# A recurrent gate beside a mixture of experts on one core: router in one run, low-rank product on VectorE, sigmoids into PSUM, first tokens on two queues

## The chip, the core and the metric

The kernel runs on one core of one Trainium2 chip. The metric is device time in microseconds, from runs of the whole program; the median of three runs of the kernel before is 840.8 us (840.55 to 841.84). A separate execution under the hardware profiler took 842.09 us.

Five engines work beside each other, each through its own row of instructions in program order: TensorE (PE in the profile, its weight loads PEld), VectorE (DVE), ScalarE (ACT), GpSimd (POOL) and SyncE (SP), which issues most transfers. They meet at semaphores. All data is 32-bit float.

## The reference

The input is 4 x 1024 tokens of 1024 values. Every token is normalised, then used twice: by a gated recurrence over the tokens of a batch entry, and by a feed-forward part with a router whose output is scattered to 8 rows. The results are multiplied and added to the input.

```
xn = layernorm(x)
# recurrence
g    = sigmoid(xn @ gate_w.T + gate_b)
u_g  = xn * g
d_lr = mean_t(u_g) @ d_lr_u @ d_lr_v / R        # R = 4
s    = G * cumsum(b * u_g / G),  G = cumprod(tanh(a))
y    = c * s + (d + d_lr) * u_g
# feed-forward
idx, gates = top 2 of softmax(xn @ wr.T), 8 experts
h    = silu(silu(xn @ w1.T) @ w3.T) @ w2.T
out  = zeros.at[idx[:, k]].add(gates[:, k] * h)  for k = 0, 1
result = x + y * silu(out)
```

The index of the scatter is the number of the expert, 0 to 7. So only the first 8 rows of the output differ from x, and the kernel needs y for these alone: the gate product is made for the first 1024 tokens only, whose mean `d_lr` wants, and all other rows of x are copied.

## The kernel before, in words

Tokens go in four groups (`sb` 0 to 3) of 1024. For each group there are products named by kind: `u` (by w1), `m` (by w3), and for group 0 also `g` (by the gate weights). Each product of 1024 x 1024 x 1024 is made by Strassen's scheme on 2 x 2 halves, with seven half products `i` = 1 to 7, and each of those again by seven small ones (`Half.step`, line 813), unless it is listed as plain (`PLAIN_G`, `PLAIN_M`), when it takes eight. A small product is four instructions of 128 x 256 into a PSUM bank (`small`, line 763), tagged X, Z or Y. TensorE does little else, while GpSimd and VectorE make the sums and differences of operands and VectorE and ScalarE take the results out of PSUM.

The order is written out by hand. `line` (lines 195 to 204) lists the half products; each gets a place (`start`), and a small product stands every two places. Everything else is put at a place with `at(place, f)` (line 176), and `run_todo` emits what is due before each small product. A function that yields a number goes on that many places later. All engines' instructions go through the class `Pinned`, which keeps them in this order on their engine; so the profile gives line 89 for nearly all of them, and one reads it by the names of tiles.

Memory: 20 blocks `b` of 128 x 2048 and 18 quarters `q` of 128 x 512 in SBUF, handed round by counts of uses. PSUM has two X banks, two Z banks, one Y bank, one small bank (`ps_sm`), and in `ps_acc` the bank `acc` of the scatter and one bank `rows`.

The parts that the change touches:

- First tokens. `load_x0` brings 256 tokens of x to SBUF, token by row, in four pieces for the first block (line 1070). `stats0` (line 236) takes mean and variance by `bn_stats`, makes diagonal matrices of means and scales, and after a lag spreads them to all partitions by products with ones (`bc`). `norm0` (line 287) then normalises the transposed tokens xT in place. `stats0(0, 0)` has a lag of 0: its products stand ahead of the first small product. Before it TensorE runs 16 products of no use (`idle`, line 1067).
- First weights. `first_weights` (line 559) loads block (0, 0) of w1 in two halves, interleaved with two pieces of xT; the block of gw is one transfer behind the second x block.
- Router. `route` (line 380) makes the logits of a group: 8 slices of the contraction x 4 parts of tokens, each a product 32 columns wide, into bank `plT`. It yields after every second slice. For group `sb` it begins at place U[5] + 2 (group 0) or U[5] - 4, U[5] being the start of half product 5 of `u`.
- Scatter. `scatter` (line 932) adds the gated rows of h of a group into `acc`; it is put six places behind the last result that it needs (line 926).
- Gating. `gated` (line 951) takes a quarter of g at a time: ScalarE's sigmoid in place, two places later VectorE's product with xn, which also gives sums for the mean.
- Differences by a spare bank. `with_bank` (line 512) has ScalarE copy one operand to `acc` or to a bank `rows`, so that VectorE's difference reads PSUM.
- Low-rank product. `recurrence` (line 982) makes the mean, then `pr` (8 products on TensorE), then `pd` (8 more), and all of y. It begins at place 25 of group 1. `rows` (line 1169) transposes y by products with the identity (`ty`) and begins 40 places before the end.

Of the kernel before, what the change touches and what calls it, by code (L numbers as in the profile page):

```python
# [10 lines left out]
F32 = mybir.dt.float32  # L11
# [5 lines left out]
P = 128  # L17
# [5 lines left out]
def kernel(  # L23
# [101 lines left out]
    NB, NQ = 20, 18  # L125
    IDLE = 16
    blocks = deque(
# [18 lines left out]
    pool.memset(eps, EPS)  # L146

    root = const.tile([P, 1], F32, tag="root", name="root")
    act.activation(root, eps, AF.Sqrt)
# [11 lines left out]
    vec_sb = const.tile([P, 5, KD], F32, tag="vec", name="vec_sb")  # L161
    lru_sb = const.tile([P, KD, R], F32, tag="lru", name="lru_sb")


# [71 lines left out]
    def stats0(I, a, xb, lag):  # L236

        mv = sp.tile([P, 2, 2], F32, tag="mv", name=f"mv_{I}{a}")
        for tt in range(2):
            xt = xb[:, 2 * tt : 2 * tt + 2, :]  # L240
            bn = sp.tile([P, 2, nc.vector.BN_STATS_DIM], F32, tag=f"bn{tt}", name=f"bn_{I}{a}{tt}")
            for n in range(2):
                dve.bn_stats(bn[:, n, :], xt[:, n, :])
            dve.bn_aggr(mv[:, tt, :], bn)
        xb.drop()
        sd = sp.tile([P, 2], F32, tag="sd2", name=f"sd_{I}{a}")
        act.activation(sd, mv[:, :, 1], AF.Sqrt, bias=eps)
        dg = quarter()

        def diagonals(s, w):  # L250
            for tt in range(2):
                dve.tensor_scalar(
                    dg[:, (2 * s + tt) * P : (2 * s + tt + 1) * P],
                    ident,
                    w[:, tt : tt + 1],
                    None,
                    ALU.mult,
                )

        diagonals(0, mv[:, :, 0])  # L260
        v = sp.tile([P, 2], F32, tag="v2", name=f"v_{I}{a}")
        dve.tensor_scalar(v, mv[:, :, 1], EPS, None, ALU.add)
        rs = sp.tile([P, 2], F32, tag="rs", name=f"rs_{I}{a}")
        scales(rs, v, sd, 2)
        diagonals(1, rs)
        if (I, a) == (1, 1):
            bc = ps_sm.tile([P, 2, Q], F32, tag="sm", name="bc_11")
        elif (I, a) == (1, 0):
            bc = ps_y.tile([P, 2, Q], F32, tag="Y", name="bc_10")
        elif a == 1:  # L270
            bc = acc.rearrange("p (s n) -> p s n", s=2)
        else:
            bc = ps_acc.tile([P, 2, Q], F32, tag="rows", name="bc_00")
        yield lag
        for s in range(2):
            pe.matmul(
                bc[:, s, :],
                ones,
                dg[:, s * Q : (s + 1) * Q],
                start=True,  # L280
                stop=True,
                skip_group_check=True,
            )
        dg.drop()
        bc0[I, a] = bc

    def norm0(I, a, J, parts=1):
        p = part(xn[0, I, J], a)
        bc = bc0[I, a]
        w = 4 // parts  # L290
        for h in range(0, 4, w):
            for s, op in ((0, ALU.subtract), (1, ALU.mult)):
                row = bc[:, s : s + 1, :].to_broadcast([P, w, Q])
                dve.tensor_tensor(p[:, h : h + w, :], p[:, h : h + w, :], row, op)

# [84 lines left out]
    def route(sb):  # L380
# [3 lines left out]
        for k in range(KD):  # L384
            J, b, kt = k // 4, k // 2 % 2, k % 2
            for g in range(4):
                I, a = g // 2, g % 2
                pe.matmul(
                    plT[g * CG : (g + 1) * CG, :],
                    wr_sb[:, k, :],  # L390
                    xn[sb, I, J][:, 2 * a + b, kt * Q : (kt + 1) * Q],
                    start=(k == 0),
                    stop=(k == KD - 1),
                )
            if k % 2:
                yield 1
        for IJ in HB:
# [60 lines left out]

    def load_w(name, KN, uses, before=()):
        t = block(uses)  # L460
        if not before:
            sync.dma_start(t.tile, weights[name][KN])
        for b, f in enumerate(before):
            f()
            sync.dma_start(t[:, b::2, :], weights[name][KN][:, b::2, :])
        return t
# [42 lines left out]

    spare = [0]  # L510

    def with_bank(out, p, q):

        def copy(j):
            spare[0] += 1
            ps = acc if spare[0] % 2 else ps_acc.tile([P, H], F32, tag="rows", name="spare")
            act.copy(ps, q[:, j])  # L520
            return ps

        ps = copy(0)
        yield 0.5
        for j in range(4):
            ahead = copy(j + 1) if j < 3 else None
            dve.tensor_tensor(out[:, j], p[:, j], ps, ALU.subtract)
            ps = ahead
            yield 0.5

    def late_sums(name, i):
# [26 lines left out]

    def first_weights(kind, name, before=()):

# [4 lines left out]

        b = {}

        def load(key, KN, uses, *before):
            b[key] = load_w(name, KN, uses, *before)

# [39 lines left out]
        off = 0 if kind == "u" else 1  # L610
        load(1, (0, 0), 2, before)
        one()
# [301 lines left out]
    def done(kind, sb, I, J, q, c):  # L914
# [5 lines left out]
        elif kind == "m":  # L920

            act.activation(c[:, q], c[:, q], AF.Silu)
            if q == 2:
                h2[I, J] = c
                if sb < NS - 1 and (I, 1 - J) in h2:
                    at(here[0] + 6, scatter, sb, [(I, 0), (I, 1)])
        elif q == 2:
            at(here[0] + 1, gated, sb, I, J, c)
# [22 lines left out]
    def gated(sb, I, J, c):  # L951

        xb = xn[sb, I, J]
        for b in range(2):
            for mt in range(2):
                m = J * 4 + b * 2 + mt

                def piece(t):
                    return t.tile.rearrange("p (a b) (m n) -> p a b m n", b=2, n=Q)[:, :, b, mt, :]

                act.activation(piece(c), piece(c), AF.Sigmoid, bias=vec_sb[:, 4, m : m + 1])
                yield 2
                dve.scalar_tensor_tensor(
                    piece(c),
                    piece(c),
                    1.0,
# [4 lines left out]
                )  # L971
                yield 0.5
        if sb == 0 and I == 0:
# [8 lines left out]
    def recurrence():  # L982

        av, bv, cv, dv = (vec_sb[:, i, :] for i in range(4))
        lrv = block()
        lrv_sb = lrv.tile.rearrange("p a n -> p (a n)")[0:R, 0:D]
        sync.dma_start(lrv_sb, lr_v)
        um = const.tile([P, KD], F32, tag="um", name="um")
        dve.tensor_reduce(um, usum, AX.X, ALU.add)
        dve.tensor_scalar(um, um, 1.0 / T, None, ALU.mult)  # L990
        yield 4
        pr = ps_sm.tile([R, 1], F32, tag="sm", name="pr")
        for k in range(KD):
            pe.matmul(pr, lru_sb[:, k, :], um[:, k : k + 1], start=(k == 0), stop=(k == KD - 1))
        yield 3
        rk = const.tile([R, 1], F32, tag="rk", name="rk")
        dve.tensor_copy(rk, pr)
        yield 4
        pd = ps_sm.tile([P, KD], F32, tag="sm", name="pd")
        for m in range(KD):  # L1000
            pe.matmul(pd[:, m : m + 1], lrv_sb[:, m * P : (m + 1) * P], rk, start=True, stop=True)
        lrv.drop()
        yield 3
        deff = const.tile([P, KD], F32, tag="deff", name="deff")
# [47 lines left out]
    def consts():  # L1052
        sync.dma_start(wr_sb, wr)
        sync.dma_start(vec_sb, vecs)
        sync.dma_start(lru_sb, lr_u)

    def copy_rows(n):
# [7 lines left out]


    idle = ps_sm.tile([P, P], F32, tag="sm", name="idle")
    for _ in range(IDLE):
        pe.matmul(idle, ones, ident, start=True, stop=True, skip_group_check=True)
    load_x0(0, 0, 4)  # L1070
    first = block(USES[0, 0] + G[0, 0])
    xn[0, 0, 0] = first
    first_weights(
        "u",
        "w1",
        [
            lambda b=b: sync.dma_start(first[:, b, :], xT[0, 0, 0, :, b, :])
            for b in range(2)
        ],
    )  # L1080
    load_x0(0, 1)
    first_weights("g", "gw")
    sync.dma_start(first[:, 2:4, :], xT[0, 0, 0, :, 2:4, :])
    at(-27, load_x0, 1, 0)
    at(-26, load_x0, 1, 1)
    at(-25, load_xn, 0, 0, 1, USES[0, 1] + G[0, 1])
    at(-16, load_xn, 0, 1, 0, USES[1, 0] + G[1, 0])
    at(-15, load_xn, 0, 1, 1, USES[1, 1] + G[1, 1])
    at(-10, lambda: stats0(0, 0, x0[0, 0], 0))
    at(-9, norm0, 0, 0, 0, 2)  # L1090
    at(-8, lambda: stats0(0, 1, x0[0, 1], 12.5))
    at(-7, lambda: stats0(1, 0, x0[1, 0], 14))
    at(4.6, norm0, 0, 1, 0)
    at(4.7, lambda: stats0(1, 1, x0[1, 1], 7.5))
    at(4.8, norm0, 0, 0, 1)
    at(5, norm0, 0, 1, 1)
    at(8, norm0, 1, 0, 0)
    at(11, norm0, 1, 0, 1)
    at(15, norm0, 1, 1, 0)
# [18 lines left out]
    for sb in range(NS):  # L1118
# [5 lines left out]
        at(U[3] - (12 if sb == 0 else 8.6), s4, "u", sb, n)  # L1124
        at(U[5] + (2 if sb == 0 else -4), route, sb)
        M = {i: start["m", sb, i] for i in range(1, 8)}
# [7 lines left out]
        if sb + 1 < NS:  # L1134
# [5 lines left out]
            for IJ in HB:  # L1140
# [5 lines left out]
                )  # L1146
    at(start["u", 1, 1] + 25, recurrence)
    first_w3()
# [121 lines left out]

    at(END - 40, rows)
    at(start["m", NS - 1, 7] + 15, scatter, NS - 1, [(0, 0), (1, 1)])
# [90 lines left out]
```

## Time and profile before

| | |
|---|---|
| median of three runs | 840.8 us |
| profiled execution | 842.09 us |
| its span, first to last instruction | 840.3 us |
| mean granted TensorE clock | 0.997 |
| TensorE busy | 828.4 us, 4143 records |
| VectorE busy | 546.2 us, 889 |
| GpSimd busy | 490.4 us, 377 |
| ScalarE busy | 242.7 us, 390 |
| transfers | 194.97 MB, mean 232 GB/s |

How to read it: times are from the span's start. A row of the timeline has start, length, engine, line, operation, the tile written and those read, shapes and a count of merged instructions; in brackets stands how long the engine was idle before, and what ended that. One 32-bit product instruction leaves two records, so `x8` is one small product. Records of products overlap, so costs on TensorE are read from start to start. SPq is SyncE's row of transfer issues; releasers are inferred from semaphores.

### The profile page before, as it was taken

What the parts mean: (1) busy time and instruction counts of PE and PEld (TensorE: products, weight loads), DVE (VectorE), ACT (ScalarE), POOL (GpSimd) and SP (SyncE); (2) the same over time, 40 slices, a digit from 0 to 9 for tenths busy, and PEclk for the clock granted to TensorE, in tenths of its full rate; (3) what the DMA queues carried; (4) which work ended last, traced back from release to release, by engine and by line L of the source; (5) the groups of instructions that cost most, each with busy time, mean ns of one, the idle gap of its engine ahead of it and who ended that gap; (6) DMA issues with size and microseconds to landing.
All of it is one profiled execution on the core that took longest, in us unless ns stands there. A gap on an engine that the chain in (4) does not pass through costs nothing.

```text
span 840.3 us, 11334 instructions
## 1 busy us (share of the span) xinstructions
PE 828.4 (99%) x4143; PEld 702.4 (84%) x4143; DVE 546.2 (65%) x889; ACT 242.7 (29%) x390; POOL 490.4 (58%) x377
## 2 busy tenths in 40 slices
PE   7999999999999999999999999999999999999997
PEld 6887888888888868888888778888888688888885
DVE  6966699888579427676897225774994246655643
ACT  0214205866121207442112225531122021220111
POOL 0379888784878768546355753743458453564500
PEclk9999999999999999999999999999999999999999
DMA  8945427622995889728966757639775646546700
GB/s 334 422 152 210 158 97 298 239 98 79 384 402 202 303 270 378 288 87 317 410 225 227 271 180 287 238 133 404 304 237 180 197 168 245 192 144 218 287 13 2
DMA packets 55679, 194.97 MB, mean 232 GB/s; under 512 B 6356, under 2 KB 9668, under 8 KB 43592
## 3 DMA queue, kind: packets, MB, share of 16 engines
q1 hardware_dynamic: 55592, 194.24, 62.7%
q8 instruction: 33, 0.54, 0.3%
q14 instruction: 22, 0.18, 0.1%
q10 hardware_dynamic: 32, 0.02, 0.0%
HBM read 171.10 MB, written 39.87 MB: 251 GB/s over the span
## 4 chain that ended last, share of the span: by engine, by line
PE 92%; DMA 3%; DVE 2%; POOL 1%; issue 1%; SPq 0%; ACT 0%; POOLq 0%; DVEq 0%
PE X_u L89 23%; PE X_m L89 20%; PE Z_u L89 12%; PE Z_m L89 11%; PE Y_u L89 6%; PE X_g L89 6%; PE Y_m L89 5%; PE Z_g L89 4%; PE acc L89 2%; PE plT L89 2%; DMA b<-in_w 2%; DVE b L89 1%; DMA w<-q 1%; POOL q L89 1%; PE Y_g L89 1%
## 5 line engine op out<-in xcount | busy, mean ns | idle before, releaser
L89 POOL TENSOR_TENSOR q<-b 128x512 f32<-128x512 f32 x144 | 198.5, 1391 | 230.7 <-DVE b L89 52.5
L89 ACT ACTIVATE b<-b 128x512 f32<-128x512 f32 (+1 forms) x152 | 105.0, 696 | 316.2 <-DVE b L89 311.4
L89 DVE TENSOR_TENSOR b<-b,b 128x512 f32<-128x512 f32 x160 | 155.6, 989 | 2.9
L89 POOL TENSOR_TENSOR q<-b,q 128x512 f32<-128x512 f32 x91 | 130.2, 1433 | 8.8 <-issue 6.7
L89 POOL TENSOR_TENSOR b<-b,b 128x512 f32<-128x512 f32 x72 | 94.8, 1342 | 35.8 <-PE X_u L89 26.4
L89 DVE TENSOR_TENSOR b<-X_u,b 128x512 f32<-128x512 f32 x87 | 59.9, 689 | 72.2 <-PE X_u L89 71.5
L89 PE MATMUL X_u<-q,q 128*128 128x256 f32 x432 | 103.0, 381 | 0.0
L89 DVE TENSOR_TENSOR b<-X_m,b 128x512 f32<-128x512 f32 x84 | 57.4, 687 | 63.7 <-PE X_m L89 63.5
L89 PE MATMUL X_m<-q,q 128*128 128x256 f32 x416 | 98.5, 380 | 0.0
L89 PEld LDWEIGHTS X_u<-q,q 128*128 128x128 f32 x432 | 81.3, 190 | 14.9 <-POOL q L89 1.7
L89 POOL TENSOR_TENSOR q<-q,b 128x512 f32<-128x512 f32 x53 | 71.9, 1358 | 34.5 <-PE X_u L89 28.8
L89 PEld LDWEIGHTS X_m<-q,q 128*128 128x128 f32 x416 | 78.8, 190 | 11.8 <-issue 0.8
L89 DVE TENSOR_TENSOR b<-b,bc 128x1024 f32<-128x1024 f32 (+1 forms) x62 | 72.8, 1178 | 6.3 <-ACT bc L89 5.3
L89 PE MATMUL X_m<-b,b 128*128 128x256 f32 x272 | 63.8, 380 | 0.8 <-POOL b L89 0.8
L89 PE MATMUL X_u<-b,b 128*128 128x256 f32 x248 | 60.4, 388 | 2.8 <-DVE b L89 2.5
L89 PEld LDWEIGHTS X_m<-b,b 128*128 128x128 f32 x272 | 51.3, 190 | 8.6 <-POOL b L89 1.2
L89 PEld LDWEIGHTS X_u<-b,b 128*128 128x128 f32 x248 | 48.1, 195 | 10.7 <-DVE b L89 3.3
L89 PE MATMUL X_u<-b,q 128*128 128x256 f32 x216 | 51.3, 380 | 0.0
L89 PE MATMUL Y_u<-b,b 128*128 128x256 f32 x216 | 51.3, 380 | 0.0
L89 PE MATMUL Z_u<-q,b 128*128 128x256 f32 x216 | 51.3, 380 | 0.0
L89 PE MATMUL Z_u<-q,q 128*128 128x256 f32 x216 | 51.0, 379 | 0.0
L89 DVE TENSOR_TENSOR b<-Z_m,b 128x512 f32<-128x512 f32 x48 | 32.8, 686 | 28.0 <-PE Z_m L89 27.7
(152 smaller groups left out, 1164.4 us busy)
## 6 DMA issues: line engine op xcount, KB each, us to landing
q<-w SPq DMA_DIRECT2D x168, 256.0 KB, 3.3
b<-in_w SPq DMA_DIRECT2D x37, 1024.0 KB, 7.1
b<-w_T SPq DMA_DIRECT2D x25, 1024.0 KB, 5.0
b<-in_xT SPq DMA_DIRECT2D x15, 1024.0 KB, 12.8
w<-q SPq DMA_DIRECT2D x56, 256.0 KB, 6.9
b<-in_x SPq DMA_DIRECT2D x12, 1024.0 KB, 6.2
w_T<-b SPq DMA_DIRECT2D x8, 1024.0 KB, 3.9
b<-in_gw SPq DMA_DIRECT2D x7, 1024.0 KB, 5.4
```

The costliest lines, as they stand in the source:

```text
L89: r = f(*args, **kwargs)
```

## The change

- Router: `route` no longer yields between slices. For groups 1 to 3 it is put at the place of the scatter of the previous group's last pair.
- Low-rank product: `pr` is made by VectorE (product with `lru_sb`, sum over slices) and one product with ones, which sums over partitions and leaves the result on all of them; `pd` by VectorE from `lr_v`, brought transposed as a constant. `recurrence` begins six places before `m` of the last group, and `rows` 24 places before the end.
- Sigmoids: `gated` writes the sigmoid to `acc` or a bank `rows`, and VectorE's product reads it there one place later. A list of free banks serves `gated` and `with_bank`, which no longer copies one piece ahead.
- First tokens: the four pieces of x are issued two by SP, two by ACT, ahead of all else. `first_tokens` replaces `stats0(0, 0)`: means and scales get a bank each, the means' product is issued before the scales are worked out, and the first half of the tokens is normalised in smaller pieces. `idle` runs 14 times, and 2 and 3 times more behind the two products. The first block of gw comes in halves among those of w1. Other `stats0` and `norm0` get other places.

```
-    IDLE = 16
+    IDLE = 14
+    x_first = block()
+    for n in range(2):
+        for t, queue in ((0, sync), (1, act)):
+            queue.dma_start(
+                x_first[:, 2 * t + n, :], x[t * P : (t + 1) * P, n * H : (n + 1) * H]
+            )
...
+    def warm(n):
+        for _ in range(n):
+            pe.matmul(idle, ones, ident, start=True, stop=True, skip_group_check=True)
+
+    def first_tokens():
...
+        for n in range(2):
+            for t in range(2):
+                dve.bn_stats(bn[t][:, n, :], x_first[:, 2 * t + n, :])
+        for t in range(2):
+            dve.bn_aggr(mv[:, t, :], bn[t])
+        x_first.drop()
+        sd = sp.tile([P, 2], F32, tag="sd2", name="sd_00")
+        act.activation(sd, mv[:, :, 1], AF.Sqrt, bias=eps)
...
+        spread(0, mv[:, :, 0])
+        warm(2)
...
+        scales(rs, v, sd, 2)
+        spread(1, rs)
+        dg.drop()
+        warm(3)
...
+        on(0, 2, 0, ALU.subtract)
+        on(0, 1, 1, ALU.mult)
+        on(1, 2, 1, ALU.mult)
+        on(2, 4, 0, ALU.subtract)
+        on(2, 4, 1, ALU.mult)
...
                     stop=(k == KD - 1),
                 )
-            if k % 2:
-                yield 1
...
+    def with_bank(out, p, q, order=(0, 1, 2, 3), swap=False):
+        for j in order:
+            yield from spare_bank()
+            n = taken[0]
+            ps = bank_tile(n)
             act.copy(ps, q[:, j])
...
             yield 0.5
+            a, b = (ps, p[:, j]) if swap else (p[:, j], ps)
+            dve.tensor_tensor(out[:, j], a, b, ALU.subtract)
+            free_banks.append(n)
...
                     at(here[0] + 6, scatter, sb, [(I, 0), (I, 1)])
+                    if I == 0:
+                        at(here[0] + 6, route, sb + 1)
...
-                act.activation(piece(c), piece(c), AF.Sigmoid, bias=vec_sb[:, 4, m : m + 1])
-                yield 2
+                yield from spare_bank()
+                n = taken[0]
+                ps = bank_tile(n).rearrange("p (a n) -> p a n", a=2)
+                act.activation(ps, piece(c), AF.Sigmoid, bias=vec_sb[:, 4, m : m + 1])
+                yield 1
                 dve.scalar_tensor_tensor(
                     piece(c),
-                    piece(c),
+                    ps,
...
-                yield 0.5
+                free_banks.append(n)
+                yield 1
...
-        pr = ps_sm.tile([R, 1], F32, tag="sm", name="pr")
-        for k in range(KD):
-            pe.matmul(pr, lru_sb[:, k, :], um[:, k : k + 1], start=(k == 0), stop=(k == KD - 1))
...
-        for m in range(KD):
-            pe.matmul(pd[:, m : m + 1], lrv_sb[:, m * P : (m + 1) * P], rk, start=True, stop=True)
+        dve.tensor_mul(uv, lru_sb, um.unsqueeze(2).to_broadcast([P, KD, R]))
+        part_r = const.tile([P, R], F32, tag="part_r", name="part_r")
+        dve.tensor_reduce(part_r, uv.rearrange("p k r -> p r k"), AX.X, ALU.add)
+        yield 12
+        pr = ps_sm.tile([P, R], F32, tag="sm", name="pr")
+        pe.matmul(pr, ones, part_r, start=True, stop=True)
+        yield 1.5
+        rk = const.tile([P, R], F32, tag="rk", name="rk")
+        dve.tensor_copy(rk, pr)
+        yield 1
+        dve.tensor_mul(uv, lrv_sb, rk.unsqueeze(1).to_broadcast([P, KD, R]))
+        pd = const.tile([P, KD], F32, tag="pd", name="pd")
+        dve.tensor_reduce(pd, uv, AX.X, ALU.add)
...
+    sync.dma_start(first[:, 0, :], xT[0, 0, 0, :, 0, :])
+    first_half("w1", 0)
+    sync.dma_start(first[:, 1, :], xT[0, 0, 0, :, 1, :])
+    first_half("gw", 0)
+    first_half("w1", 1)
     load_x0(0, 1)
+    first_half("gw", 1)
     sync.dma_start(first[:, 2:4, :], xT[0, 0, 0, :, 2:4, :])
...
-    at(-10, lambda: stats0(0, 0, x0[0, 0], 0))
-    at(-9, norm0, 0, 0, 0, 2)
-    at(-8, lambda: stats0(0, 1, x0[0, 1], 12.5))
-    at(-7, lambda: stats0(1, 0, x0[1, 0], 14))
-    at(4.6, norm0, 0, 1, 0)
-    at(4.7, lambda: stats0(1, 1, x0[1, 1], 7.5))
-    at(4.8, norm0, 0, 0, 1)
-    at(5, norm0, 0, 1, 1)
-    at(8, norm0, 1, 0, 0)
-    at(11, norm0, 1, 0, 1)
+    at(-10, first_tokens)
+    at(-8, lambda: stats0(0, 1, x0[0, 1], 12.4))
+    at(4.6, lambda: stats0(1, 0, x0[1, 0], 4.800000000000001))
+    at(4.5, norm0, 0, 1, 0)
+    at(8, lambda: stats0(1, 1, x0[1, 1], 6))
+    at(6, norm0, 0, 0, 1)
+    at(9, norm0, 0, 1, 1)
+    at(10, norm0, 1, 0, 0)
+    at(12, norm0, 1, 0, 1)
...
-        at(U[5] + (2 if sb == 0 else -4), route, sb)
+        if sb == 0:
+            at(U[5] + 2, route, sb)
...
-    at(start["u", 1, 1] + 25, recurrence)
+    at(start["m", NS - 1, 1] - 6, recurrence)
...
-    at(END - 40, rows)
+    at(END - 24, rows)
```

## The prediction

> **What bounds the kernel now.** I read the busy shares of the page first, then its chain of work that ended last.
>
> ```profile
> PE 828.4 (99%) x4143; PEld 702.4 (84%) x4143; DVE 546.2 (65%) x889; ACT 242.7 (29%) x390; POOL 490.4 (58%) x377
> PE 92%; DMA 3%; DVE 2%; POOL 1%; issue 1%; SPq 0%; ACT 0%; POOLq 0%; DVEq 0%
> ```
>
> TensorE is busy for 99% of the span and carries 92% of the chain, so an edit is worth time only if it shortens TensorE's own instructions, starts its first real product earlier, or removes one of its stalls. Busy time hides slow stretches, so next I read TensorE's timeline by starts. A full product of four 128x256 instructions (eight records) takes 344.59 - 342.86 = 1.73 us, and nearly all follow each other at that step. What is over 1.73 from start to start is loss. Three places show it.
>
> The router in the timeline of TensorE:
>
> ```profile
> 71.48 1.99 PE L89 MATMUL Z_g<-b,b 128*128 128x256 f32 x8
> 73.31 1.89 PE L89 MATMUL Z_u<-q,q 128*128 128x256 f32 x8
> 75.13 1.07 PE L89 MATMUL plT<-b,wr_sb 128*32 128x256 f32 x16
> 76.13 1.99 PE L89 MATMUL X_g<-b,b 128*128 128x256 f32 x8
> 78.05 1.07 PE L89 MATMUL plT<-b,wr_sb 128*32 128x256 f32 x16
> ```
>
> Z_u before plT takes 75.13 - 73.31 = 1.82, that is 0.09 too long; X_g between two parts takes 1.92, 0.19 too long; plT itself takes 1.00. A part so costs 1.20 us.
>
> The low-rank product:
>
> ```profile
> 338.74 1.89 PE L89 MATMUL X_u<-b,b 128*128 128x256 f32 x8
> 340.56 0.54 PE L89 MATMUL pr<-um,lru_sb 128*4 128x1 f32 x16
> 341.03 1.99 PE L89 MATMUL X_u<-q,q 128*128 128x256 f32 x8
> 342.86 1.89 PE L89 MATMUL Z_u<-q,q 128*128 128x256 f32 x8
> 344.59 1.89 PE L89 MATMUL Z_u<-q,b 128*128 128x256 f32 x8
> ...
> 351.49 1.89 PE L89 MATMUL X_u<-b,b 128*128 128x256 f32 x8
> 353.31 1.94 PE L89 MATMUL pd<-rk,b 4*128 4x1 f32 x16
> 355.19 1.99 PE L89 MATMUL X_u<-q,q 128*128 128x256 f32 x8
> 357.02 1.24 PE L89 MATMUL Z_u<-q,q 128*128 128x256 f32 x5
> ```
>
> The start, in the timeline of all engines and then in windows (columns: length, busy of PE, PEld, DVE, ACT, POOL, TensorE's clock, DMA share, GB/s):
>
> ```profile
> 7.65 0.69 DVE L89 BATCH_NORM_STATS2 bn<-b 128x6 f32<-128x512 f32 x1 [1.18 <-DMA b<-in_x]
> 11.01 2.73 DVE L89 TENSOR_TENSOR b<-b,bc 128x512 f32<-128x512 f32 x4 [0.79 <-PE bc L89]
> 12.48 5.41 PE L89 MATMUL X_u<-b,b 128*128 128x256 f32 x16 [1.50 <-DVE b L89]
> ```
>
> ```profile
> 3.00:6.00 3.00, 3.00 (x17) 3.00 (x16) 1.82 (x4) 0.00 (x0) 0.00 (x0) 1.00 0.69 235
> 9.30:12.70 3.40, 1.31 (x5) 0.52 (x4) 2.47 (x8) 0.00 (x0) 0.00 (x0) 1.00 1.05 424
> 12.70:16.10 3.40, 3.40 (x9) 2.69 (x9) 3.33 (x7) 0.00 (x0) 0.00 (x0) 0.50 1.01 418
> ```
>
> The first real product waits until 12.48 for a chain that hangs on the fourth piece of x; then the clock is 0.50 for 3.4 us, after a stretch in which TensorE had little to do. The waits by engine name the stalls that are left:
>
> ```profile
> PE X_u L89 <- DVE b L89: 2.5, 2, 1.5
> PE X_m L89 <- POOL b L89: 0.8, 1, 0.8
> ```
>
> **The change, part by part.**
>
> Router. The order of instructions shows the 32 products of each group of 1024 tokens in a row, four times, where they stood in four parts. The number of products is the same. In a run, each further quarter costs four steps of 0.216 (1.73 / 8) = 0.86 us, not 1.20: three quarters x 0.34 = 1.0 us per group. For groups 1 to 3 the run stands behind the second scatter (acc), where the second part stood before, so that pair's saved switch is there in both. Four groups: 4.0 us. The tokens are normalised by then: the part that stands first now starts later than before. Bounds 3.4 to 4.1 (a drain inside the run; the switch all gone).
>
> Low-rank product. Out go pr (341.03 - 338.74 - 1.73 + 342.86 - 341.03 - 1.73 = 0.66) and pd (355.19 - 351.49 - 1.73 + 357.02 - 355.19 - 1.73 = 2.07), 2.7 us. In comes one product of 128x4 against the ones; nearest is ta (128x8), four records 0.54 to the next: two records, 0.2. Net 2.5 (2.2 to 2.6). VectorE gets two multiplications and two reductions over 32 elements per row; rows of that size took 0.16 to 0.22, up to 0.95 when one waited beside GpSimd (the product "first" at 364.44). Some 2 us of VectorE, which is busy 65%; hidden by the 12 places (some 20 us) between them and the TensorE product that needs them. They move from the second group to the last one. At 363.92 one X eviction stood behind "first" and TensorE lost 2.17 - 1.73 = 0.44; in the last group there are no gating products and no norms, so I count 0.3 (0 to 0.4). What is late next if the chain is late: the transposes of y (ty), which stand in TensorE's row; between the chain's end and them are about 7 places, 12 us. One small transfer (lr_v) moves to the constants near 50 us; 0.33 of SP's queue, with nothing waiting on it there.
>
> Start. x comes in four pieces by two queues; in the kernel before SP issues all four ahead of xT (0.74 to 2.60, 0.46 each), in the changed one two. So the last piece of x, xT and the first half of w1 are issued 0.93 us earlier. Here a rule of the Trainium skill speaks against more: DMA: Bandwidth & Descriptors, "Issuing engines are not separate DMA queues", says that a second issuing engine only saves the time of issuing, since both feed the same 16 DMA engines. The row speaks for more: at 3 to 6 us those engines were only 0.69 busy at 235 GB/s, against 424 later, so they waited for work, and 0.25 MB at 424 GB/s would take 0.6 us where pieces 3 and 4 came 1.9 us apart. By the rule the last piece lands at 6.7; by the row as early as 5.2. I take the rule. From landing to first product it was 12.48 - 7.65 = 4.83. Now the two last pieces come together, so one more statistics instruction stands behind them (+0.64) and both aggregates (+0.13); but the means' product is off early, the first subtraction (0.69) follows the diagonal at once instead of after the 0.79 wait, and TensorE starts after a half scale (0.37, half of 0.69 plus fixed time): 0.79 + 0.69 - 0.37 = -1.1. So 4.5, and X_u starts at 11.2: 1.3 us. By the row it would start at 9.7: 2.8. The first half of w1 (landed 9.53) sets 8.6 as the floor. A half of gw now stands ahead of w1's second half and of x's next block (+1.27 us at 0.52 MB, less 0.93): that block lands near 14.4 rather than 14.10; its statistics then end near 17.7 (3.3 us, as 14.97 to 18.27), and TensorE asks for them at 11.2 + 6.9 = 18.1. Tight, no stall.
>
> Clock. The idle product runs 14 + 2 + 3 times, not 16. Between 9.3 and 12.7 TensorE will have the scales (0.43), three idle (0.67) and X_u from 11.2 (1.5) rather than 0.9 of real issue, so the 0.50 stretch should not come: eight records at 0.216 rather than 0.43, 1.7 us. The other rule weighed: TensorE: Matmul & The Clock Gate, "What's actually happening", says that the window of 3.4 us that decides this is free-running, so that the same kernel may fall on another phase. The trace's change at 12.70 is one such edge. By the rule the 1.7 may be had or half lost in any run: start 1.3 to 3.0. I take 1.7, as any window now has more work. Start together: 3.0 (0.5 to 4.5).
>
> Sigmoids. They go to a PSUM bank, and the gating product reads it there: 16 at 0.69 (as rows with one PSUM operand, X_g 685 ns) rather than 1029 ns. Four table loads fewer stand in ScalarE's order (25, not 29, 1.28 each), off the path. It counts where VectorE was behind: X_u at 171.53 came 2.89 after its forerunner, not 1.73, with its bank freed by VectorE at 171.48. In the 16 us before it four gating products took 4.5 us, now 2.8. That is more than the 1.16 (+0.1) of stall, but each now follows its sigmoid by one place rather than two and can block VectorE's row, evictions of X and Z behind it. I take 0.8 (-2 to 1.26).
>
> The rest (norms re-timed in the first 30 us, y's rows 16 places later) lies beside TensorE, under products that it has anyway. If the statistics of block (1,1) come late, their spread stalls TensorE by up to 1; they end about 1 us ahead.
>
> Sum: 4.0 + 2.5 + 0.3 + 3.0 + 0.8 = 10.6. The profiled execution took 842.09 (span 840.3): 831.5. The median 840.8 is 1.3 below it, so 830.2.
>
> **Rivals.**
> 1. The start gains little: the DMA engines were slow in themselves from 3 to 6 us, X_u starts near 12.2, and the sparse stretch moves ahead and costs clock elsewhere. 0.5 in place of 3.0: 832.7. For: every piece there was slow. Against: the idle products now fill the gaps.
> 2. The sigmoids give back 3 us: VectorE waits for ScalarE, which has squares of 1.14 and table loads of 1.28 in its row. 834.
> 3. Slower: the same wait in earnest. A gating product can find a table load, a silu, a square and its sigmoid ahead (1.28 + 0.63 + 1.14 + 0.72 = 3.8). TensorE's two X banks shelter about 1.7. It decides when the unsheltered waits of the 16 pass 11.4 us (10.6 less the 0.8 counted), 0.7 each; at 0.9 each, 14.4: 843.8. Against: before, VectorE waited for these only 1.3 us in all.
>
> **How the numbers follow.** Forecast 0.56, start lost 0.26, sigmoids 0.11, slower 0.06, 0.01 for no difference. 0.2% (1.7 us) is what a measurement here can tell. Faster 0.93, same 0.01, slower 0.06. The likeliest case spans 828.3 to 832.2 (start 4.5, or stall and router at their low ends). Low end 827.5: start at 4.5 and the gating stall gone with 1.26. High end 835: rival 1 with 2 of rival 2. About 0.15 is left out.
>
> **What would show it.** plT as four rows of 64 records; no pr of 16, no pd. X_u before 11.5 and no window at 0.50 after it. No stall near 165 over 0.5. Wrong if VectorE's waits for ScalarE at the gating products grow past 5 us, if X_u starts after 12, or if a spread of statistics holds TensorE near 18 or 35.

## The result, and the profile after

The changed kernel takes 838.12 us (median of 7 runs, 837.39 to 839.15); the kernel before took 841.29 beside it (7 runs, 839.74 to 843.35). The ratio is 0.9962, with a 95% interval of 0.9949 to 0.9975: 3.2 us faster, where 10.6 were forecast. The profiled execution took 839.15, with a span of 837.4 us.

Most steps of the forecast came in. What took 8 us back is one small instruction on VectorE that no step had given a price. First the busy shares and the chain of work that ended last, from the page of the changed kernel:

```profile
PE 823.4 (98%) x4119; PEld 704.2 (84%) x4119; DVE 549.7 (66%) x894; ACT 236.8 (28%) x386; POOL 484.8 (58%) x377
...
PE 95%; DVE 2%; DMA 2%; issue 0%; ACT 0%; SPq 0%
```

TensorE is busy 5 us less than before, but its share fell from 99% to 98%: there is idle time in the span that was not there. The router and the low-rank product are as forecast, here in TensorE's timeline (start, length, then the instruction and how many records):

```profile
68.59 3.66 PE L89 MATMUL plT<-b,wr_sb 128*32 128x256 f32 x64
72.18 1.99 PE L89 MATMUL Z_g<-b,b 128*128 128x256 f32 x8
...
741.72 0.28 PE L89 MATMUL pr<-part_r,ones 128*128 128x4 f32 x2
741.86 1.97 PE L89 MATMUL Y_m<-b,b 128*128 128x256 f32 x8
```

The run of 64 records takes 72.18 - 68.59 = 3.59 us from start to start, against four parts of 1.00 and four pairs of switches; pr takes 0.14. Next the start, in the timelines of TensorE and VectorE, and in windows (columns as in the prediction: length, busy of PE, PEld, DVE, ACT, POOL, TensorE's clock, DMA share, GB/s):

```profile
10.38 4.02 PE L89 MATMUL X_u<-b,b 128*128 128x256 f32 x16
14.24 1.89 PE L89 MATMUL X_g<-b,b 128*128 128x256 f32 x8
15.97 1.89 PE L89 MATMUL Z_u<-b,b 128*128 128x256 f32 x8
18.26 0.70 PE L89 MATMUL acc<-q,ones 128*128 128x256 f32 x2 [0.40 <-DVE q L89]
19.61 0.70 PE L89 MATMUL acc<-q,ones 128*128 128x256 f32 x2 [0.66 <-DVE q L89]
```

```profile
5.66 1.29 DVE L89 BATCH_NORM_STATS2 bn<-b 128x6 f32<-128x512 f32 x2 [0.36 <-DMA b<-in_x]
14.93 1.29 DVE L89 BATCH_NORM_STATS2 bn<-b 128x6 f32<-128x512 f32 x2 [2.58 <-DMA b<-in_x]
```

```profile
3.00:6.00 3.00, 3.00 (x16) 3.00 (x15) 1.63 (x3) 0.17 (x1) 0.00 (x0) 1.00 1.00 332
9.30:12.70 3.40, 3.19 (x17) 2.45 (x16) 2.25 (x5) 0.00 (x0) 0.00 (x0) 1.00 1.05 417
```

The last piece of x is there at 5.66, two microseconds earlier than before, and X_u starts at 10.38. Its 16 records take 3.86 and not 5.24, since the clock stays at 1.00. Some 1.5 us go back at once: TensorE now comes to the spread of the second block's statistics (acc), of which x lands at 14.93, before VectorE has it, and waits on each half of it.

Then comes a place that had no stall before. TensorE's timeline, VectorE's, GpSimd's and ScalarE's, each around 90 us:

```profile
93.23 1.89 PE L89 MATMUL Z_g<-q,b 128*128 128x256 f32 x8
101.06 3.78 PE L89 MATMUL X_u<-b,b 128*128 128x256 f32 x8 [5.94 <-ACT b L89]
104.63 2.25 PE L89 MATMUL X_g<-b,q 128*128 128x256 f32 x8
```

```profile
87.13 11.72 DVE L89 CAST ixf<-ix 128x16 f32<-128x16 uint32 x1
98.77 0.16 DVE L89 TENSOR_TENSOR df<-mx 128x8 f32<-128x8 f32 x1
98.85 0.68 DVE L89 TENSOR_TENSOR b<-Y_g,b 128x512 f32<-128x512 f32 x1
```

```profile
86.51 1.30 POOL L89 TENSOR_TENSOR q<-b,q 128x512 f32<-128x512 f32 x1
87.73 4.98 POOL L89 TENSOR_TENSOR b<-b,b 128x512 f32<-128x512 f32 x4
92.63 1.31 POOL L89 TENSOR_TENSOR q<-b 128x512 f32<-128x512 f32 x1
93.85 1.31 POOL L89 TENSOR_TENSOR b<-b,b 128x512 f32<-128x512 f32 x1
95.08 1.30 POOL L89 TENSOR_TENSOR q<-b,q 128x512 f32<-128x512 f32 x1
96.30 2.52 POOL L89 TENSOR_TENSOR b<-b,b 128x512 f32<-128x512 f32 x2
```

```profile
98.96 0.31 ACT L89 ACTIVATE g<-df 128x8 f32<-128x8 f32 x2 [12.99 <-DVE df L89]
100.43 0.58 ACT L89 COPY b<-X_u 128x512 f32<-128x512 f32 x1
```

Read them from the bottom. TensorE's X_u waits for ScalarE to copy an X bank out (100.43). ScalarE had been idle for 12.99 us, because the sigmoid of df stands ahead of that copy in its row, and df stands behind the CAST. The CAST turns 16 indices per partition into f32. It takes 0.16 us in the other three groups; here it takes 11.72, and it ends at 98.85, which is when GpSimd's unbroken row of subtractions ends (96.30 + 2.52 = 98.82). The line that names the wait ("ACT b") so names the last of four links, not the cause.

From start to start Z_g takes 7.83 us and not 1.73: 6.1 us lost. The next two products are slow as well, 3.57 and 2.09, which is 2.2 more. The windows show why:

```profile
93.20:98.50 5.30, 1.92 (x9) 1.33 (x8) 5.30 (x1) 0.00 (x0) 5.30 (x5) 1.00 0.99 325
98.50:105.40 6.90, 4.34 (x10) 3.53 (x11) 4.72 (x14) 1.01 (x4) 0.32 (x1) 0.51 0.11 40
105.40:110.00 4.60, 4.60 (x23) 4.03 (x22) 0.86 (x2) 1.59 (x3) 0.00 (x0) 1.00 0.45 120
```

After TensorE had done nothing from about 95 on, its clock was 0.50 for 6.8 us from 98.5 on, so the stall was paid for a second time: 8.3 us in all. 3.2 + 8.3 = 11.5, which is what the forecast's steps together should have given, and a little more.

In the kernel before, the same CAST met the same row of GpSimd and waited for one instruction only. Its lines in the timelines of VectorE and GpSimd:

```profile
96.49 1.23 DVE L89 CAST ixf<-ix 128x16 f32<-128x16 uint32 x1
```

```profile
95.97 1.72 POOL L89 TENSOR_TENSOR q<-b 128x512 f32<-128x512 f32 x1
```

GpSimd's subtraction took 1.72 there and not 1.3: a gating product with only SBUF operands (scalar_tensor_tensor, b<-b,b, at 95.89) had got in just ahead of it. So the change moved the CAST 9.4 us ahead (the last plT ends 9.8 earlier, 2 of it by the earlier start and the rest by the one run). It also took away the gating products that had broken GpSimd's row; whether that had a part in it is not shown, since a later run that keeps them (b_router) starves as well.

### The profile page after: what moved, and what is told of

Its sections match the earlier page's. It is cut to its first block, busy times and chain, and to the rows that moved or that the text cites. A ratio compares the mean times of both kernels' runs of the same rounds, so it can differ in the third digit from the quotient of the medians.

```text
span 837.4 us, 11277 instructions
## 1 busy us (share of the span) xinstructions
PE 823.4 (98%) x4119; PEld 704.2 (84%) x4119; DVE 549.7 (66%) x894; ACT 236.8 (28%) x386; POOL 484.8 (58%) x377
## 4 chain that ended last, share of the span: by engine, by line
PE 95%; DVE 2%; DMA 2%; issue 0%; ACT 0%; SPq 0%
PE X_m L89 23%; PE X_u L89 23%; PE Z_m L89 12%; PE Z_u L89 12%; PE Y_u L89 6%; PE X_g L89 5%; PE Y_m L89 5%; PE Z_g L89 4%; PE acc L89 2%; PE plT L89 2%; DMA b<-in_x 2%; DVE ixf L89 1%; PE Y_g L89 1%; PE pp L89 0%; DVE bn L89 0%; DVE b L89 0%
## 5 line engine op out<-in xcount | busy, mean ns | idle before, releaser
L89 POOL TENSOR_TENSOR q<-b 128x512 f32<-128x512 f32 x144 | 196.3, 1376 | 232.5 <-DVE b L89 63.2
L89 DVE TENSOR_TENSOR b<-b,b 128x512 f32<-128x512 f32 x160 | 157.4, 1000 | 2.9
L89 POOL TENSOR_TENSOR q<-b,q 128x512 f32<-128x512 f32 x91 | 128.3, 1413 | 10.7 <-issue 8.5
L89 DVE TENSOR_TENSOR b<-b,bc 128x1024 f32<-128x1024 f32 x56 | 67.7, 1211 | 5.5 <-ACT bc L89 5.4
## 6 DMA issues: line engine op xcount, KB each, us to landing
b<-in_gw SPq DMA_DIRECT2D x6, 1024.0 KB, 13.8
```

The source lines that it names most:

```text
L89: r = f(*args, **kwargs)
```

## The experiments

To starve is here to wait while one GpSimd instruction after the other goes ahead. The theory, T: the router's CAST starves on VectorE behind GpSimd's row, as a copy from SBUF to SBUF, and what it holds up behind it costs the 8 us. T2 is its wider form: every VectorE instruction with only SBUF operands starves there. The first rival, R1, blames the sigmoids: ScalarE and the spare banks. Times of the kernel before are those run on the same chip beside each group of experiments.

**The CAST on another engine, in another form, and later** (three edits of the changed kernel; before: 840.90).

```diff
-        dve.tensor_copy(ixf, ix[:, :, 0:2])
+        act.copy(ixf, ix[:, :, 0:2])
```

> The changed kernel, with the router's CAST of the expert indices (ixf<-ix, 128x16) on ScalarE instead of VectorE. Theory T: in the first group's router that small cast, a copy from SBUF to SBUF, starved on VectorE for 11.7 us behind GpSimd's unbroken row, and other forms wait for one GpSimd instruction at most (1.3 us, as oh in the kernel before); so df waits at most 1.3 us, X_u at 101 comes near 95, the clock stays at 1.00 there, and the time falls by 7 to 9 us from 838.1 to 829 to 831. Theory T2: every VectorE instruction with only SBUF operands starves there; df, next in the row, takes some 11.6 us and the time stays at 838. Rival R1: the stall is ScalarE's, from the sigmoids into spare banks; it stays and the time is 838.

```diff
-        dve.tensor_copy(ixf, ix[:, :, 0:2])
+        dve.tensor_tensor(ixf, ix[:, :, 0:2], ix[:, :, 0:2], ALU.max)
```

> The changed kernel, with the cast kept on VectorE at its place, but as a TENSOR_TENSOR with two SBUF inputs (max of ix with itself, written as f32), the form of df and oh. T: it waits for one GpSimd instruction at most (up to 1.3 us), the stall at 93 to 101 is gone or below 1 us, time 829 to 831. T2: it starves as the cast did, some 11.7 us, time 838. R1: 838, the stall stays.

```diff
+        if sb == 0:
+            yield 8
         dve.tensor_copy(ixf, ix[:, :, 0:2])
```

> The changed kernel, with the first group's cast and all that follows it in the router 8 places (some 14 us) later, so that it meets the time in which GpSimd has nothing to do (98.8 to 113.5). T and T2: the cast takes under 0.5 us, no stall at 93 to 101, clock 1.00 there, time 829 to 831. R1: the wait of ScalarE and the stall stay, time 838.

Measured: 837.71 (ratio 0.9966, 0.9953 to 0.9978), 838.66 (0.9977, 0.9967 to 0.9987) and 830.59 (0.9885, 0.9868 to 0.9901). VectorE's timeline in the first, the second and the third:

```profile
86.23 11.71 DVE L89 TENSOR_TENSOR df<-mx 128x8 f32<-128x8 f32 x1
```

```profile
86.06 11.72 DVE L89 TENSOR_TENSOR ixf<-ix 128x16 f32<-128x16 uint32 x1
```

```profile
99.46 0.17 DVE L89 CAST ixf<-ix 128x16 f32<-128x16 uint32 x1
```

T in its first form (only a copy starves) is false: with the CAST gone, df takes its place and its 11.7 us. T2 holds for the two that took its place, each an operation on two SBUF operands. As it is worded it is too wide: the eight maxima and index searches just ahead of the CAST also have only SBUF operands, and none waits, though GpSimd works without a pause from 79.13 on. One pair in VectorE's timeline of the changed kernel, and GpSimd's row over it:

```profile
84.28 0.16 DVE L89 FIND_INDEX8 ix<-mx,lg 128x8 uint32<-128x8 f32 x1
84.36 0.15 DVE L89 MAX8 mx<-lg 128x8 f32<-128x8 f32 x1
```

```profile
84.04 1.31 POOL L89 TENSOR_TENSOR b<-b,b 128x512 f32<-128x512 f32 x1
```

In all the traces these two take 0.15 to 0.17 us, 64 of them in each. So what is left of T2 is: two SBUF operands, or a copy within SBUF (a tensor_scalar of 128x2 within SBUF, at 324.34, waited as well, for 1.1 us; none was seen to starve). R1 is false as well, because the sigmoids and their banks are the same in the third kernel and the stall is gone. What is left there of lost time is 1.1 us near 118, where X_u waits for VectorE; two of the one-hot operations now wait 1.3 each beside GpSimd's next row.

**The same place and engine, with one operand in PSUM.** Only the operands of the first group's small operations change.

```diff
+            sm = ps_sm.tile([P, 19, N8], F32, tag="sm", name="small_0")
+            ixf = sm[:, 0:2, :].rearrange("p j t -> p t j")
+            second = sm[:, 2, :]
+            oh = sm[:, 3:19, :].rearrange("p (j t) e -> p j t e", j=2)
+            dve.tensor_copy(second, mx[:, :, 1])
...
-        dve.tensor_sub(df, mx[:, :, 0], mx[:, :, 1])
+        dve.tensor_sub(df, mx[:, :, 0], second)
...
```

> The changed kernel, with the first group's small operations at their place and on VectorE, but with one operand of each (the indices as f32, the second maximum, the one-hot rows) in a PSUM bank, so that none has only SBUF operands. T2 (what starves is an instruction that has only SBUF operands, in reach of GpSimd's row): the cast takes some 0.2 us at 86 to 87, the stall of TensorE at 93 to 101 is gone, the clock stays at 1.00 there, 829 to 831. If VectorE as a whole is held up in that stretch, whatever its operands, the stall stays and the time is 838.

Measured: 829.42 (four executions, 829.05 to 829.59), against 841.33 for before (0.986, 0.9844 to 0.9877). VectorE's timeline, in the same stretch of GpSimd's row:

```profile
85.86 0.17 DVE L89 COPY small<-mx 128x8 f32<-128x8 f32 x1
86.06 0.18 DVE L89 CAST small<-ix 128x16 f32<-128x16 uint32 x1
86.27 0.17 DVE L89 TENSOR_TENSOR df<-mx,small 128x8 f32<-128x8 f32 x1
```

None waits, and TensorE has no stall there (Z_g to X_u: 91.96 to 93.69, 1.73). This is the clean test of T2 as narrowed: same engine, same moment, same sizes, 0.18 for 11.72. It also gives the price of the starving in whole runs: 838.12 - 829.42 = 8.7.

**Each part of the change alone, on the kernel before.** The edits are the hunks of the diff: route in one run and its two calls (b_router); gated and with_bank (b_sigmoid); first_tokens, the loads ahead and the re-timed norms (b_start); recurrence, lrv_sb and the place of rows (b_lowrank).

```diff
-            if k % 2:
-                yield 1
```

> The kernel before with the router's part of the change alone (32 products of a group in one run). Without a stall it is 4.0 us faster than before (841.3 to 837.3). T and T2: the cast now comes some 8 us earlier, near 88, into GpSimd's row that lasts to 102 here; if it starves to the end of the row, TensorE loses some 8 us or more and the time is 845 or above. R1 (sigmoids to blame): no stall, 837.3.

```diff
-                act.activation(piece(c), piece(c), AF.Sigmoid, bias=vec_sb[:, 4, m : m + 1])
-                yield 2
...
+                act.activation(ps, piece(c), AF.Sigmoid, bias=vec_sb[:, 4, m : m + 1])
+                yield 1
```

> The kernel before with the sigmoids' part of the change alone (the gating product reads the sigmoid from a PSUM bank). The prediction's step: 0.8 us faster (2 slower to 1.3 faster), 840.1. T2: the gating products no longer meet GpSimd (so the stall of 1.2 near 170 is gone), but the cast at 96.5 is left with GpSimd's row to 102: if it starves there, up to 6 us are lost, 842 to 846. R1 (VectorE waits for ScalarE at the banks): 2 to 4 us slower, without a long cast.

```diff
+    at(-10, first_tokens)
```

> The kernel before with the start's part alone (first tokens by two queues, their means off early, norms re-timed). The prediction's step: 3.0 us (0.5 to 4.5), 837.9. By the trace of the changed kernel: X_u 2.1 earlier, its products 1.4 shorter, 1.5 lost at the spread of the second block's statistics: 2.0, so 838.9.

```diff
-    at(start["u", 1, 1] + 25, recurrence)
+    at(start["m", NS - 1, 1] - 6, recurrence)
```

> The kernel before with the low-rank product's part alone (two multiplications and reductions on VectorE, one product of 128x4, the recurrence in the last group). The prediction's steps: 2.5 and 0.3, so 2.8 us faster than before, 838.5; pr 0.14 in the trace of the changed kernel makes it 2.6 to 3.1.

| part alone | before beside it | measured | ratio (95%) | forecast step |
|---|---|---|---|---|
| router | 840.90 | 854.70 | 1.0164 (1.0147 to 1.0181) | 4.0 faster |
| sigmoids | 841.33 | 839.14 | 0.9978 (0.9969 to 0.9988) | 0.8 faster |
| start | 841.33 | 838.56 | 0.9965 (0.9954 to 0.9976) | 3.0 faster |
| low-rank | 841.62 | 837.38 | 0.9952 (0.9935 to 0.9968) | 2.8 faster |

The router's part alone is 13.8 us slower than no change, and it isn't the CAST that starves in it. VectorE's and TensorE's timelines:

```profile
80.68 20.22 DVE L89 SCALAR_TENSOR_TENSOR b<-b,b 128x512 f32<-128x512 f32 x1 [1.35 <-ACT b L89]
```

```profile
103.14 3.78 PE L89 MATMUL Y_g<-b,b 128*128 128x256 f32 x8 [15.07 <-DVE b L89]
```

A gating product starved for 20.2 us, to the end of GpSimd's row at 100.3, and TensorE lost 15.1. With the sigmoids alone it is the CAST again, for 4.73 us, but there TensorE shows no wait: by the timelines the X bank that it asked for at 102.78 had been emptied by 101.9. VectorE's timeline of that run:

```profile
95.76 4.73 DVE L89 CAST ixf<-ix 128x16 f32<-128x16 uint32 x1
```

So each of two parts brings the starving on by itself, at two different instructions. What it costs depends on how long the wait is and on what stands behind the starved one.

**What decides whether an instruction starves.** Elsewhere in all these traces a VectorE instruction with two SBUF operands, or a copy within SBUF, that meets GpSimd's row waits 1.2 us at most and gets in at the next border between two GpSimd instructions. Nothing lies between these and the waits of 3.4 us and more that are called starving here. Four edits of the changed kernel ask why not here.

```diff
-        pool.memset(c, 0.0)
+        (dve if sb == 0 else pool).memset(c, 0.0)
```

> The changed kernel, with the first group's memset of C on VectorE instead of GpSimd. In all four runs in which an instruction starved, GpSimd's row had a memset ahead of the starved one and no VectorE instruction had got in since. Theory T3: that memset changes who gets its turn; without it the cast waits for one GpSimd instruction at most (1.3 us) and the time is 829 to 831. T2 without that: the cast still takes 10 us or more, 837 to 839.

```diff
+            for k in range(4):
+                at(U[5] + 2.6 + 2 * k, dve.tensor_tensor, t8, ids, ids, ALU.max)
```

> The changed kernel, with four more small VectorE instructions that have only SBUF operands (128x8, into a tile that nothing reads), some 3.5 us apart, in the first group's stretch from 73 us on, ahead of the cast at 87. Theory T4: an instruction gets in at the next border between two GpSimd instructions while the row is young or was broken lately (all of those seen with 13 or fewer unbroken GpSimd instructions since the last break waited 1.2 us at most), and starves once the row has run long without a break (17 to 24 instructions in the starved cases). The four then wait 1.2 us each at most and keep the row broken, the cast waits 1.2 us at most, and with 4 operations and waits more than the changed kernel it takes 829 to 832. If age has no part in it and place or phase decide, the first of them or the cast starves as before: 838, or 850 and more if the first one does (26 us of row ahead).

```diff
...
+            if eng is pool:
+                used.append(h)
+                pool.memset(tiny[:, len(used) - 1 : len(used)], 0.0)
```

> The changed kernel, with a memset of one column (128x1, into a tile that nothing reads) on GpSimd behind each of its subtractions of whole blocks (b<-b,b), 9 of them in the row from 84 to 99; the cast stays at 87 on VectorE with SBUF operands. In the last run an instruction that had starved from 74.2 got in at 77.8, just as GpSimd came to a memset, which reads nothing. Theory T5: GpSimd keeps the way to SBUF from one reading instruction to the next where they follow without a pause, and an instruction that reads nothing lets VectorE in. Then the cast ends with the next memset, near 89 (2 us at most), the stall of 7.8 and the 0.50 clock behind it are gone, 829 to 831. If a memset does nothing for it, the cast takes some 11 us as before: 838.

```diff
+            if eng is pool:
+                pool.memset(accT, 0.0)
```

> As the run before, with a memset of 128x256 (0.3 us, as that of C) in the place of one of 128x1 (88 ns); it writes a tile that is cleared again before it is used. The cast had starved over four of the short ones. If the length of GpSimd's pause from reading decides (T5 with a length), the cast ends with the first such memset, near 89, and the time is 829 to 832 (GpSimd's row is 2.5 us longer). If the kind of GpSimd's instruction has no part in it, as the memset of C in one run, in which nothing got in (b_router), suggests, the cast starves to the end of the row, now near 101, and the time is 840 or more.

Measured: 837.76 without GpSimd's memset (0.9966, 0.9956 to 0.9976; the CAST takes 11.5), so T3, that this memset settles whose turn it is, is false. With the short memsets 838.79 (0.9977, 0.9967 to 0.9986), so T5, that an instruction of GpSimd which reads nothing lets VectorE in, is false in that form. VectorE's and GpSimd's timelines with them:

```profile
85.54 12.03 DVE L89 CAST ixf<-ix 128x16 f32<-128x16 uint32 x1
```

```profile
86.24 1.25 POOL L89 TENSOR_TENSOR b<-b,b 128x512 f32<-128x512 f32 x1
87.44 0.09 POOL L89 MEMSET tiny<- 128x1 f32 x1
```

The CAST let six such memsets pass (not four, as the expectation of the longer ones has it). With memsets of 0.30 us the time is 839.82 (0.9988, 0.9977 to 0.9999). There df and the next eviction are recorded from 88.36 and 88.44, at the first long memset, and both end with the row at 99.97. That may mean that the CAST got in at that memset and df starved in its place; the CAST's own record runs to 99.97 too, so this run is inconclusive on length. It is clear only that a memset doesn't take the stall away.

The four extra instructions gave what was least expected: five executions of one program took 847.35, 842.84, 829.43, 829.34 and 829.29. In the profiled one, the slowest of them, VectorE's and GpSimd's timelines have:

```profile
74.21 3.58 DVE L89 TENSOR_TENSOR t<-ids 128x8 f32<-128x8 f32 x1
...
78.92 18.68 DVE L89 TENSOR_TENSOR t<-ids 128x8 f32<-128x8 f32 x1
```

```profile
76.47 1.29 POOL L89 TENSOR_TENSOR q<-q,b 128x512 f32<-128x512 f32 x1
77.69 0.33 POOL L89 MEMSET C<- 128x256 f32 x1
```

The first of the four waited over three GpSimd instructions until the memset of C, the second from 78.92 to the end of the row, and TensorE then lost 15.2 us. T4, that only a row which has long run without a break makes an instruction starve, is false in the profiled execution: the first was 8 instructions past the last break, and the second came 1.1 us after the first had got in. The three executions near 829.4 have no trace, but their time is the one without the stall, and their mean clock was 0.998 to 1.000, against 0.988. So, by these times, the same instruction at the same place in the program starves in one execution and not in the next. What decides at the border is left open. Two things are shown: the starved one gets in at the latest when GpSimd's row ends, and neither the place in the row nor the form of the instruction nor a memset settles it.

**The best version.** One operand in PSUM, and the spread of the second block's statistics one place later.

```diff
-    at(-8, lambda: stats0(0, 1, x0[0, 1], 12.4))
+    at(-8, lambda: stats0(0, 1, x0[0, 1], 13.4))
-    at(4.5, norm0, 0, 1, 0)
+    at(5.5, norm0, 0, 1, 0)
```

The third block's statistics move from 4.6 to 5.6, and their lag from 4.8 to 3.8.

> The changed kernel with the first group's small operations on a PSUM operand (as in the run that gave 829.4), and the spread of the second block's statistics, its norm and the third block's statistics one place later, so that TensorE has a product of 1.73 us before it. That run lost 0.55 us between the two halves of that spread; it should come back: 828.9. If the norm that follows comes too late for the product that needs it, 829.4 to 830.5.

Measured: 828.99, against 841.62 (0.9859, 0.9842 to 0.9875), with a span of 827.2. TensorE's timeline at the place that had lost 1.5 us:

```profile
17.42 1.89 PE L89 MATMUL X_g<-b,b 128*128 128x256 f32 x8
19.15 1.03 PE L89 MATMUL acc<-q,ones 128*128 128x256 f32 x4
20.01 1.89 PE L89 MATMUL Z_u<-b,b 128*128 128x256 f32 x8
```

The four records take 0.86 with no wait. This version is 9.1 us faster than the changed kernel and 12.6 faster than the one before. The 0.4 us over the version with the PSUM operand alone is too small to be sure of by the intervals, but the wait is gone from the trace.

## Why the prediction was right or wrong

*Router, 4.0: right on TensorE, and the step that failed.* The four runs take 3.59, 3.57, 3.57 and 3.57, as forecast. But the step counted TensorE's products alone. The router is a chain: its products, then eight maxima and indices, the CAST, df, the sigmoids, the one-hot rows. To put the products in one run moved all of that some 9 us ahead on VectorE, and the sum put it at nothing without a reason: the step doesn't name the chain, and the paragraph on "The rest" has only the norms and y's rows. In its place the runs showed a CAST that starved for 11.7 us and held evictions up behind it. Price: 8.7 us, so the router's term is -4.7 and not 4.0 in this kernel, and -13.8 alone. The prediction had a hint of it in hand: it quoted 0.95 for a small instruction that waited beside GpSimd, and used it for the low-rank product only. That the CAST would meet GpSimd's row at its new time could be read from the lines of before. The size could not: no such wait in the profile before is over 1.2 us.

A page would have given a wrong comfort here. The Trainium skill, "SBUF — State Buffer", section "SBUF: two separate sides", says that VectorE and GpSimd share one pair of ports, held for a whole instruction by whoever starts first, and that a VectorE instruction takes part in it with two SBUF inputs (against a GpSimd instruction that reads SBUF) or in a two-port mode, into which a plain f32 copy within SBUF falls. Which instructions took part agrees with these runs: the CAST, df and the gating product with SBUF operands did; those with a PSUM operand did not (0.18). Read as it stands, the rule makes the wait what is left of one GpSimd instruction, at most 1.3 by the durations here. Most waits here are just that, but the measured one went on over nine further instructions; of what happens at the border between two of them the rule as quoted says nothing.

*Low-rank product, 2.5 and 0.3: right, and the 4.2 that it gave alone (2.7 to 5.5 by the interval) is in part luck.* Its own terms in the trace are 2.5 (pr 0.14 and one switch of 0.08, for 0.66 + 2.07) and the stall of 0.44 that is gone. Another 0.9 is the clock: in its profiled execution the first 16 records took 4.30 and not 5.24, with the kernel's old start and without the 0.50 stretch. Nothing in this part touches the start, so this fits the free-running window that the prediction weighed: the same start on another phase. Some 0.3 is left over.

*Start, 3.0: right in size, through larger terms of both signs.* X_u came 2.1 earlier, not 1.3. The rule of the issuing engines had put it at 11.2, the row at 9.7; it came at 10.38. From 3 to 6 us the DMA engines were 1.00 busy at 332 GB/s, against 0.69 and 235, so the issues that came earlier did fill time in which they had waited for work; no run changes the second queue alone. The clock gave 1.4 of the 1.7, and that is no luck of the phase: of the four traces with the old start three have the 0.50 stretch near 12, of the eleven with the new one none. Then "Tight, no stall" failed: TensorE, ahead of its time, waited 1.5 us for the second block's statistics in this profile, 0.6 in b_start, and 0.5 at least in each trace with this order. The term that was mis-sized is the 3.3 us from landing to the end of the statistics. It was read from the first aggregate (14.97) and not from the first statistics instruction, which in the kernel before starts at 13.66: 13.66 to 18.27 is 4.6, and 14.93 to 19.56 in the changed kernel is 4.6 again. The condition was named ("if a spread of statistics holds TensorE near 18 or 35"), but the sum gave it no price.

*Sigmoids, 0.8: right in sign, too small.* Alone they gave 2.2. The stall near 170 is gone (1.2, of which 0.8 was taken), and so is one of 1.0 near 240, where X_m had waited for GpSimd. The likely link, argued from the durations and not tested: gating products with SBUF operands had held GpSimd up, 1.7 us for a subtraction of 1.3. The prediction showed that wait of X_m and didn't connect it. The range's bad end, VectorE waiting for ScalarE, did not come: its waits for the two banks that ScalarE fills are 2.4 and 1.9 us in all.

*The rivals.* None of the three came. Rival 3 was of the right kind, a VectorE instruction that waits unsheltered with the evictions behind it, but it named ScalarE as the one waited for, and 0.9 us sixteen times instead of 11.7 once.

Without the starving the steps add to 4.0 + 2.9 + 3.3 + 2.2 = 12.4 by the traces (start: 2.2 + 1.7 - 0.6, from b_start's), against 11.9 measured (841.33 to 829.42). Two ends of the prediction's ranges do not come out of the terms that it names: from 830.2, a start of 4.5 gives 828.7 and not 828.3, and with the gating stall gone as well 828.2 and not 827.5.

## What to carry to other kernels

Before you move a step, list what it issues on every engine, and lay each VectorE instruction that has two SBUF operands, or copies within SBUF, against GpSimd's row at the new time and not at the old one: a row of GpSimd without a pause can hold a 0.2 us instruction for as long as the row lasts. If such an instruction stands ahead of evictions, put one of its operands in PSUM or place it where GpSimd is idle. And read a stall from its last link backwards: here TensorE's wait named ScalarE, ScalarE's named VectorE, and only the end times named GpSimd.

## What the runs showed of the hardware that was not expected

A VectorE instruction of 16 elements took 11.72 us and a gating product 20.22 us, until GpSimd's row of 1.3 us instructions ended; the same waits were 1.2 at most elsewhere. Five executions of one program took 829.3 to 847.4 us, and the slowest has a wait of 18.68 in its trace. Two SBUF operands, or a copy from SBUF to SBUF, were exposed to it; the same operations with an operand in PSUM took 0.17 to 0.23 in the same stretch, and maxima and index searches from SBUF to SBUF, with GpSimd at work all the while, 0.15 to 0.17.

Memsets by GpSimd between its reading instructions, of 0.09 or 0.30 us, did not take the stall away (838.79 and 839.82 us).

TensorE's clock fell to 0.50 within its stall of 6 us and stayed there for 6.8 us, 4.3 of them past the stall's end; with that, 6.1 us lost became 8.3. In b_router, with a stall of 15 us, it was 0.50 for 17.1 us, 4.5 of them past the end.
